# End of a sparse attention kernel: the last reciprocals' transpose ahead of the last context group, and the output chunks finished in another order

## The chip, the cores and the metric

One core of one Trainium2 chip runs the whole kernel in one launch. The metric is device time in microseconds (us) of the launch. TensorE (PE in the profile) does the matrix products, VectorE (DVE) and ScalarE (ACT) the elementwise work, GpSimd (POOL) issues the indirect transfers, SyncE (SP) the plain ones.

## The reference

For each of 16 batches of 1024 tokens with 512 features the kernel computes masked self-attention with one shared projection for queries, keys and values, and adds it to its input:

```python
xt = jnp.transpose(x, (0, 2, 1))                     # (16, 1024, 512)
q = xt @ Wq.T
qh = q.reshape(B, T, NH, dk).transpose(0, 2, 1, 3)   # 8 heads of 64
scores = scale * jnp.einsum('bhqd,bhkd->bhqk', qh, qh)
logits = (scores * cmask + (1.0 - cmask) * NEG) * rmask
attn = jax.nn.softmax(logits, axis=-1)
ctx = jnp.einsum('bhqk,bhkd->bhqd', attn, qh)
out = ctx.transpose(0, 2, 1, 3).reshape(B, T, D) @ Wo.T
return x + jnp.transpose(out, (0, 2, 1))
```

The mask holds zeros and ones and differs by batch; about half of the tokens are active. A row of a masked token has all logits equal, so its context is the mean of all queries.

## The kernel before, in words

The kernel gathers the active tokens of a batch into 512 to 544 slots and computes attention among those only; the masked tokens get one common row per batch, added in a pass of its own (line 888). All tokens go back to `y_out` by scatters, indirect transfers that POOL issues (line 901), 128 rows of 2 KB each.

Per batch, with the heads in four pairs p = 0 to 3:

- `scores` (line 701 for the products) computes a block of 128 queries against all slots for a head, and ScalarE takes the exponential and its row sums `z` (line 705).
- `attend` (line 726) multiplies the exponentials with the values. The context of one head pair is collected in one PSUM tile `pav`; the last 16 products of a pair are the context group, after which ScalarE copies the tile out as `c` (line 734).
- `recip_sums` (lines 749 to 758, DVE) makes the reciprocals of the row sums as columns in `rcol`. `recip_rows` turns them into rows: a TensorE transpose by the identity (line 764), a DVE copy `rr` out of PSUM (line 767), a small transfer to device memory `rd` (line 769, SP), and two transfers that read it back spread over 64 partitions each, `rb` (line 773, SP).
- `norm` (lines 799 to 803, DVE) multiplies `c` with `rb` and splits the result into two float16 parts, high and low, for the output product. In the last batch these are `xh` and `xl`.
- `product` (line 817) is the output product: for a chunk of 128 slots and each head pair e, three TensorE products (high x high weights, high x low weights, low x high weights), so twelve to a chunk. `plus` (line 822, DVE) adds the sum to the gathered input rows `xa`, and `scatter` sends them away.

Batches overlap: while batch b has its scores computed, the projections of b+1 and the output of b-1 are put between them by a list of pieces with costs (`run`). After the last batch nothing is left to overlap with, and `last` writes the end out by hand. Before the change it does this, in this order: the context group of the last head pair and all transfers still waiting; `recip_sums` of pair 3; the products of all four chunks for e = 0 to 2, nine for each chunk, with `recip_rows` behind chunk 0's; `norm` of pair 3; then for each chunk the three products for e = 3, `plus` and `scatter`. The four chunks' sums lie in two PSUM tiles `pss`, chunks 0 and 1 in the first and 2 and 3 in the second.

This is the order in which the program is written. A scheduler then orders each engine's instructions by priority and readiness as it expects them. `high_priority` moves a piece ahead, and `issue_after` (the helper `behind`, line 344) holds it behind a named instruction in that order, without a wait at run time. In the order that the scheduler built before the change TensorE does three products of chunk 0 (e = 0), the context group, the other six of chunk 0, the transpose of line 764, and nine each for chunks 1, 2 and 3; then for e = 3 the high products of chunks 0 and 2, the low ones of both, then chunk 1 and chunk 3. The order of `plus` and of the scatters is chunks 0, 2, 1, 3. Waits between engines are placed by tile: an instruction that writes any part of a tile waits for the earlier readers of the tile.

At the very end every engine loads a flag (line 1272) and branches (line 1273) over a general version of the kernel that is not executed with these inputs; POOL drains its transfers and the engines meet (line 1298).

Of the kernel before, what the change touches and what calls it, by code (L numbers as in the profile page):

```python
# [19 lines left out]
P = 128  # L20
# [5 lines left out]
DC = D // P  # L26
# [17 lines left out]
HPO = 300  # L44


class Fast:
# [344 lines left out]
    def rows(self, idx, tile):  # L392
        n = idx.shape[0]
        with self.behind(*self.pool):
            dma = self.nc.gpsimd.indirect_dma_start(out=tile[:n], out_offset=None, in_=self.x,  # L395
                                                    in_offset=bass.IndirectOffsetOnAxis(ap=idx, axis=0))
        self.once(dma, self.beat)
        self.pool = [dma.ins]
        return tile
# [360 lines left out]
    def recip_rows(self, b, p):  # L760

        nc, s = self.nc, self.st[b]
        pt = self.pm([P, P])
        nc.tensor.transpose(pt, self.rcol[p % 2], self.ident)
        rr = self.sb([10, P], F32, "rr", 2)
        with self.tc.high_priority(offset=HPO):
            nc.vector.tensor_copy(rr, pt[:10])
        rd = self.dram.tile([10, P], F32, tag="rd", name="rd")
        nc.sync.dma_start(out=rd, in_=rr)
        A = s["A"]  # L770
        rb = self.sb([P, C], F32, "rb", 2)[:, :A]
        for k in range(2):
            nc.sync.dma_start(out=rb[k * DK:(k + 1) * DK, :], in_=rd[5 * k:5 * k + 5, :].rearrange("k t -> (k t)")[:A]
                              .unsqueeze(0).broadcast_to([DK, A]))
        s.setdefault("rb", {})[p] = rb
# [33 lines left out]
    def product(self, ch, cl, cols, po=None, es=range(DC)):  # L809

        nc = self.nc
        if po is None:
            po = self.pm([P, D])
        wh, wl = self.w["o"]
        for e in es:
            for k, (a, w) in enumerate(((ch, wh), (ch, wl), (cl, wh))):
                nc.tensor.matmul(po[:cols.stop - cols.start], lhsT=a[:, e, cols], rhs=w[:, e, :],  # L817
                                 start=(e == 0 and k == 0), stop=(e == DC - 1 and k == 2))
        return po

    def plus(self, x, po):
# [88 lines left out]

    def last(self, b, todo):

        for f in self.soon + todo:
            f()
        self.soon = []
        while self.urgent or self.spare:
            self.issue()
        self.paced = False
        s = self.st[b]
        self.recip_sums(b, 3)  # L920
        pos = []
        for i in range(2):
            t = self.ps_s.tile([P, 2, D], F32, tag="s", name="pss")
            pos += [t[:, k, :] for k in range(2)]
        for i in range(4):
            self.product(s["ch"], s["cl"], slice(i * P, (i + 1) * P), pos[i], range(3))
            if i == 0:
                self.recip_rows(b, 3)
        self.norm(b, 3)
        for i in range(4):  # L930
            self.project(b, i, pos[i], range(3, DC))

    def run(self, flag):
        B = self.B
# [368 lines left out]
```

## Time and profile before

| what | us |
|---|---|
| median of three timed runs | 1032.48 |
| the three runs | 1032.48, 1032.27, 1036.74 |
| the profiled execution, its own time | 1036.56 |
| its span in the profile | 1034.9 |
| TensorE busy | 989.3 (96% of the span) |
| DVE busy | 724.1 (70%) |
| ACT busy | 659.2 (64%) |
| POOL busy | 301.5 (29%) |
| POOL's last scatter starts, after the span's start | 1029.88 |

The span is what the profile records from the first to the last instruction of one execution; the execution's own time is 1.66 longer. Starts in the timeline are counted from the span's start, and a line there reads: start, duration, engine, line of the kernel, operation, what it writes and reads, count; in brackets, how long the engine idled before it and what ended that. A name with q, as SPq or POOLq, is an engine's queue of transfers or its sequencer. TensorE's products are pipelined: a 128x512 product is recorded with 0.38 though one follows the other by about 0.22. The view of stretches gives for each one the engines' busy time with the number of instructions, then TensorE's granted clock as a share of full speed, the DMA engines' busy share and GB/s.

### The profile page before, as it was taken

The page shows a single profiled execution, that of the slowest core. Times are in us where ns is not written, and L with a number is a line of the kernel's source. Part 1 is how long each engine was busy: PE and PEld are TensorE (multiplying, and loading weights), DVE is VectorE, ACT ScalarE, POOL GpSimd, SP SyncE. Part 2 cuts the span into 40 slices and gives each one's busy share as a digit, 9 for nine tenths or more (in the row PEclk, how much of TensorE's full clock was granted, in tenths as well). Part 3 has the DMA queues.
Part 4 walks back from the last instruction along what each step waited for, and adds up shares of the span by engine and source line. Part 5 has one row for each costly group of instructions (what it writes and reads, how often), then busy time and mean ns, then how long its engine had stood idle before and what let it go on. Part 6 is the DMA issues. An engine that isn't in the chain of part 4 may idle for free. (4 is left out here: it accounts for less than half of the span.)

```text
span 1034.9 us, 23506 instructions
## 1 busy us (share of the span) xinstructions
PE 989.3 (96%) x8455; PEld 686.2 (66%) x8455; DVE 724.1 (70%) x2410; ACT 659.2 (64%) x1702; POOL 301.5 (29%) x307
## 2 busy tenths in 40 slices
PE   7798999999999999999999999999999999999996
PEld 6576667666676766767666676766767666676563
DVE  6897668676675667876676787767677776666653
ACT  5876667657667665667667567666667666565550
POOL 3101013222311232333232333323233232326562
PEclk9899999999999999999999999999999999999998
DMA  6846556557654485575658665576665657455652
GB/s 206 224 135 184 139 137 162 174 160 205 175 133 131 138 244 167 154 208 142 197 158 217 181 174 170 155 202 187 164 211 147 195 166 193 140 142 186 195 187 85
DMA packets 78795, 177.73 MB, mean 172 GB/s; under 512 B 14688, under 2 KB 20576, under 8 KB 78672
## 3 DMA queue, kind: packets, MB, share of 16 engines
q1 hardware_dynamic: 57584, 108.40, 39.0%
q0 software_dynamic: 21088, 67.75, 20.9%
q8 instruction: 69, 1.13, 0.5%
q14 instruction: 54, 0.44, 0.1%
HBM read 91.49 MB, written 33.91 MB: 121 GB/s over the span
## 5 line engine op out<-in xcount | busy, mean ns | idle before, releaser
L705 ACT ACTIVATE p<-pss,nm 128x528 f32<-128x528 f32 (+2 forms) x512 | 359.3, 706 | 186.5 <-PE pss L701 176.6
L701 PE MATMUL pss<-xx 128*128 128x264 f16 (+2 forms) x2048 | 302.7, 277 | 6.3 <-ACT p L705 5.2
L726 PE MATMUL pav<-p,v 128*64 128x264 f32 (+2 forms) x2048 | 243.3, 390 | 0.0
L701 PEld LDWEIGHTS <-xx 128*128 128x128 f16 x2048 | 194.9, 99 | 64.2 <-issue 26.2
L726 PEld LDWEIGHTS pav<-p,v 128*64 128x64 f32 x2048 | 141.5, 137 | 85.6 <-issue 13.5
L901 POOL DMA_INDIRECT y_out<-xa,idx x68 | 73.5, 1081 | 282.3 <-PE pss L701 100.1
L513 PE MATMUL pm<-xh,wqh 128*128 128x264 f16 (+5 forms) x512 | 142.4, 278 | 3.7 <-DVE xa L822 3.1
L513 PE MATMUL pm<-xh,wql 128*128 128x264 f16 (+5 forms) x512 | 141.9, 277 | 0.0
L513 PE MATMUL pm<-xl,wqh 128*128 128x264 f16 (+5 forms) x512 | 141.8, 277 | 0.0
L395 POOL DMA_INDIRECT xa<-x_in,idx x68 | 67.4, 992 | 208.2 <-PE pss L701 91.8
L513 PEld LDWEIGHTS <-wqh 128*128 128x128 f16 x1024 | 98.3, 99 | 23.7 <-issue 7.1
L705 ACT ACTIVATION_READ_ACCUMULATOR p<-pss,nm 128x1 f32 x512 | 104.1, 203 | 0.0
L901 POOL DMA_INDIRECT y_out<-xi,idx x60 | 73.6, 1226 | 96.7 <-PE pss L701 27.6
L817 PE MATMUL pm<-woh,ch 128*128 128x512 f16 x240 | 91.1, 380 | 0.0
L817 PE MATMUL pm<-wol,ch 128*128 128x512 f16 x240 | 91.0, 379 | 0.0
L817 PE MATMUL pm<-woh,cl 128*128 128x512 f16 x240 | 91.0, 379 | 0.0
L395 POOL DMA_INDIRECT xi<-x_in,idx x60 | 62.5, 1042 | 93.6 <-PE pss L701 31.2
L516 ACT ACTIVATE q<-pm 128x264 f32<-128x264 f32 (+5 forms) x128 | 50.1, 391 | 58.1 <-PE pm L513 57.4
L822 DVE SCALAR_TENSOR_TENSOR xa<-pm,xa 128x512 f32<-128x512 f32 x60 | 41.3, 688 | 54.3 <-PE pm L817 50.6
L817 PEld LDWEIGHTS <-ch 128*128 128x128 f16 x480 | 46.0, 98 | 44.8 <-issue 0.9
L888 DVE TENSOR_TENSOR xi<-xi,ub 128x512 f32<-128x512 f32 (+1 forms) x60 | 40.8, 687 | 42.6 <-PE pss L701 42.3
L799 DVE TENSOR_TENSOR c<-c,rb 128x528 f32<-128x528 f32 (+2 forms) x64 | 45.4, 709 | 30.0 <-PE pm L513 16.3
(223 smaller groups left out, 1506.4 us busy)
## 6 DMA issues: line engine op xcount, KB each, us to landing
xx<-hl SPq DMA_DIRECT2D x224, 136.0 KB
xm<-x_nat_in SPq DMA_DIRECT2D x56, 512.0 KB
rb<-rd SPq DMA_DIRECT2D x72, 132.0 KB
rb<-rd SPq DMA_DIRECT2D x40, 136.0 KB
pt<-c SPq DMA_DIRECT2D x36, 132.0 KB
pt<-p SPq DMA_DIRECT2D x36, 132.0 KB
ub<-ud SPq DMA_DIRECT2D x16, 256.0 KB
xx<-hl SPq DMA_DIRECT2D x32, 128.0 KB
```

The source lines that it names most:

```text
L395: dma = self.nc.gpsimd.indirect_dma_start(out=tile[:n], out_offset=None, in_=self.x, in_offset=bass.IndirectOffsetOnAxis(ap=idx, axis=0))
L513: self.beat = nc.tensor.matmul(pq, lhsT=w[:, c, e * P:(e + 1) * P], rhs=xx[:, c, cols], start=(k == 0), stop=(k == 3 * DC - 1)).ins
L516: nc.scalar.activation(s["q"][:, e, cols], pq, AF.Copy, scale=1.0 / (SX * SW))
L701: self.beat = nc.tensor.matmul(pt[:, g, :CH], lhsT=xx[:, 2 * k, i * P:(i + 1) * P], rhs=xx[:, 2 * k + a, g * CH:(g + 1) * CH], start=(a == ...
L705: self.exp = [nc.scalar.activation(t.rearrange("p (g c) -> p g c", g=2), pt[:, :, :CH], AF.Exp, bias=s["nm"][p // HG][:, p % HG:p % HG + 1 ...
L726: mm = nc.tensor.matmul(s["pav"][k * DK:(k + 1) * DK, g, :CH], lhsT=s["v"][p][:, i, k * DK:(k + 1) * DK], rhs=ps[k][:, cols], start=(i == ...
L799: self.once(nc.vector.tensor_tensor(c[:, :A], c[:, :A], s["rb"][p], ALU.mult), self.beat if p < 3 else None)
L817: nc.tensor.matmul(po[:cols.stop - cols.start], lhsT=a[:, e, cols], rhs=w[:, e, :], start=(e == 0 and k == 0), stop=(e == DC - 1 and k == 2))
L822: self.nc.vector.scalar_tensor_tensor(x, po, 1.0 / (SX * SW), x, ALU.mult, ALU.add)
L888: self.once(self.nc.vector.tensor_tensor(x[:n], x[:n], s["ub"][:n], ALU.add), self.beat)
L901: dma = self.nc.gpsimd.indirect_dma_start(out=self.out, out_offset=bass.IndirectOffsetOnAxis(ap=idx, axis=0), in_=x, in_offset=None)
```

## The change

Only `last` is rewritten, and two other functions keep a handle on the instruction that they issued last.

- `recip_sums` and `recip_rows` of pair 3 and the first six products of chunk 0 get high priority, and are written ahead of the last context group; `recip_rows` is held behind the sixth product, the context group and what else is left of the batch behind the transpose.
- Chunk 0's last three products for e = 2 and chunk 1's nine for e = 0 to 2 follow; chunks 2 and 3 get none at this point.
- After `norm`, chunks 0 and 1 are finished with e = 3. Chunks 2 and 3 are held behind them and computed in one piece each, all twelve products and then `plus` and `scatter`.

The number of instructions is the same on each engine. In the built order of the changed kernel TensorE does nine products of chunk 0, the transpose, the context group, nine of chunk 1, then for e = 3 chunk 0 and chunk 1, then twelve of chunk 2 and twelve of chunk 3. `plus` and the scatters go in the order 0, 1, 2, 3. Nothing else moves on any engine.

```diff
@@ recip_rows
-        nc.tensor.transpose(pt, self.rcol[p % 2], self.ident)
+        self.turn = nc.tensor.transpose(pt, self.rcol[p % 2], self.ident).ins
@@ product
-                nc.tensor.matmul(po[:cols.stop - cols.start], lhsT=a[:, e, cols], rhs=w[:, e, :],
-                                 start=(e == 0 and k == 0), stop=(e == DC - 1 and k == 2))
+                self.mm = nc.tensor.matmul(po[:cols.stop - cols.start], lhsT=a[:, e, cols], rhs=w[:, e, :],
+                                           start=(e == 0 and k == 0), stop=(e == DC - 1 and k == 2)).ins
@@ last
-        for f in self.soon + todo:
+        s = self.st[b]
+        rows = lambda i: slice(i * P, (i + 1) * P)
+        for f in self.soon:
             f()
         self.soon = []
-        while self.urgent or self.spare:
-            self.issue()
-        self.paced = False
-        s = self.st[b]
-        self.recip_sums(b, 3)
         pos = []
         for i in range(2):
             t = self.ps_s.tile([P, 2, D], F32, tag="s", name="pss")
             pos += [t[:, k, :] for k in range(2)]
-        for i in range(4):
-            self.product(s["ch"], s["cl"], slice(i * P, (i + 1) * P), pos[i], range(3))
-            if i == 0:
+        with self.tc.high_priority(offset=HPO):
+            self.recip_sums(b, 3)
+            self.product(s["ch"], s["cl"], rows(0), pos[0], range(2))
+            with self.behind(self.mm):
                 self.recip_rows(b, 3)
+        with self.behind(self.turn):
+            for f in todo:
+                f()
+        while self.urgent or self.spare:
+            self.issue()
+        self.paced = False
+        self.product(s["ch"], s["cl"], rows(0), pos[0], range(2, 3))
+        self.product(s["ch"], s["cl"], rows(1), pos[1], range(3))
         self.norm(b, 3)
-        for i in range(4):
+        for i in range(2):
             self.project(b, i, pos[i], range(3, DC))
+        with self.behind(self.mm):
+            for i in range(2, 4):
+                self.project(b, i, pos[i])
```

## The prediction

> **What bounds the kernel now.** The page comes first: TensorE is busy 96% of the span and 9 tenths or more in nearly every slice until the last, where its digit is 6. The change touches only the program's end; in the built order of both kernels every engine's instructions are the same up to the last batch's end. So I read the timeline from 1010 us on, then the DMA rows, then TensorE's granted clock. The timeline of before, cut to the chain of the last head pair's reciprocals (start, us, engine, line):
>
> ```profile
> 1011.77 3.67 PE L726 MATMUL pav<-p,v 128*64 128x256 f32 x32
> ...
> 1012.55 0.17 DVE L758 TENSOR_TENSOR rcol<-rcol,hit 128x10 f32<-128x10 f32 x1
> ...
> 1016.68 0.27 PE L764 MATMUL pm<-ident,rcol 128*128 128x128 f32 x1
> ...
> 1017.00 0.28 DVE L767 COPY rr<-pm 10x128 f32<-10x128 f32 x1 [4.27 <-PE pm L764]
> ...
> 1017.30 0.31 SPq L769 DMA_DIRECT2D rd<-rr  x1
> ...
> 1018.51 1.27 SPq L773 DMA_DIRECT2D rb<-rd  x2
> ...
> 1022.23 0.69 DVE L799 TENSOR_TENSOR c<-c,rb 128x512 f32<-128x512 f32 x1 [4.95 <-SPq L1273]
> ```
>
> The reciprocals are ready at 1012.72 (1012.55 + 0.17) but transposed at 1016.68, behind the context group and six products. From there two DMAs in a row, rd then rb, end at 1022.23 (SP's L1273 merely stands where rb landed). Then the end, PE, DVE and POOL of the same timeline:
>
> ```profile
> 1023.83 0.39 PE L817 MATMUL pss<-woh,xh 128*128 128x512 f16 x1 [1.04 <-DVE xh L802]
> ...
> 1024.70 0.60 PE L817 MATMUL pss<-woh,xl 128*128 128x512 f16 x2
> ...
> 1025.86 0.38 PE L817 MATMUL pss<-woh,xh 128*128 128x512 f16 x1 [0.57 <-DVE xa L822]
> ...
> 1025.12 1.29 DVE L822 SCALAR_TENSOR_TENSOR xa<-pss,xa 128x512 f32<-128x512 f32 x2 [0.62 <-PE pss L817]
> 1026.71 1.34 DVE L822 SCALAR_TENSOR_TENSOR xa<-pss,xa 128x512 f32<-128x512 f32 x2 [0.30 <-PE pss L817]
> ...
> 1026.08 0.96 POOL L901 DMA_INDIRECT y_out<-xa,idx  x1 [12.51 <-DVE xa L822]
> 1027.35 0.96 POOL L901 DMA_INDIRECT y_out<-xa,idx  x1 [0.30 <-issue]
> 1028.61 0.96 POOL L901 DMA_INDIRECT y_out<-xa,idx  x1 [0.30 <-issue]
> 1029.88 0.96 POOL L901 DMA_INDIRECT y_out<-xa,idx  x1 [0.31 <-issue]
> ```
>
> Once the first chunk is added (L822), POOL is the bound: four scatters 1.27 apart, the last at 1029.88. POOL's own drain ends at 1034.05, the span at 1034.9. So the end is the last scatter's start + 5.02.
>
> **The change part by part.** *The transpose moved up.* In the built order TensorE now does nine products of chunk 0 (e = 0 to 2), the transpose L764, the context group L726, nine products of chunk 1. Products follow each other by 0.216 (1021.33 to 1022.41: five steps in 1.08). Nine from 1011.03 end at 1012.97; their last operand is written at 1011.17 (L803, 1010.49 + 0.68) and rcol is ready at 1012.72, so nothing holds them. L764 starts at 1012.97 instead of 1016.68: **3.71 earlier**. The context group starts 0.20 behind it (as at 1001.24 to 1001.44), at 1013.17, 1.40 later than now; ScalarE's copy of it, 1015.49 now, ends at 1017.47. That is hidden behind rb, which lands later; without this cover it would cost 1.40. Chunk 1's nine products run from 1016.78 to 1018.72.
>
> *The two DMAs moved with it.* On SP they stand behind the same flag load as before (1012.1 to 1012.85); the copy rr would end at 1013.57, so SP is free. POOL's queue is unchanged. New is company: the scatter that POOL issues at 1012.60 still moves data (193 and 262 GB/s in 1013 to 1015; 16 GB/s after). From rd to rb SP waited 1.21 in the quiet (above), 1.45 at 994.23 just behind one scatter, 3.69 at 953.49 among several. I take 1.45, the row with one scatter: 0.24 lost. From rb to the multiply L799 it is 3.72 in the quiet and 5.20 among gathers (971.23 to 976.43); the scatter is over by then, so 3.72. L799 starts at T = 1022.23 - 3.71 + 0.24 = **1018.76**.
>
> *The end reordered.* Before, twelve products are left at T, three for each chunk; the other nine of chunks 2 and 3 ran while rd and rb were under way. Now they follow chunk 1, so thirty products stand behind T: 18 more, 18 x 0.216 = 3.9 of TensorE that lose their cover. The wait counts of the built program name two holds: chunk 1's first product behind T waits for chunk 0's L822, as it does now at 1025.86, and, new on this path, **chunk 3's first of all waits for chunk 2's L822**, because both chunks are halves of one tile. Queued behind these waits are all later products, and DVE and POOL behind them. From T, with before's own steps:
> - first product T + 1.60 (1023.83 - 1022.23); xl, written at T + 2.26, product at T + 2.40 (between 2.32 and 2.47);
> - L822 starts 0.42 after its last product (1024.70 to 1025.12) and takes 0.65: T + 2.82 to 3.47; POOL 0.31 later;
> - chunk 1 starts 0.09 after that (1025.77 to 1025.86), T + 3.56; its L822 T + 4.41 to 5.06, POOL T + 5.37, more than 1.27 after the first;
> - chunk 2 follows; its last product is 14 x 0.216 after T + 3.56, T + 6.58; L822 T + 7.00 to 7.65;
> - chunk 3 from T + 7.74, last product T + 10.12; L822 T + 10.54 to 11.19; **last scatter T + 11.50**.
>
> Before, the last scatter was T + 7.65 (1029.88 - 1022.23). So the end costs **3.85**, against 3.71 - 0.24 = 3.47 gained: + 0.38.
>
> *The tail* is kept at 5.02. The last scatter now goes alone; before, the last one's data flowed from about 1030.84 to 1032.2, and 256 KB at the 262 GB/s of 1030 to 1031 take 0.98, so between 0 and 0.4 may be gained; I take 0. The branch out of the program hides beside it: TensorE's takes 4.06 from 1027.0 and starts once the last hold is passed, about 1026.4 in both; DVE's drain comes 4.5 after the last L822 starts (1027.4 to 1031.9), so at 1033.8, against POOL's 1034.4: a cover of 0.6.
>
> **Sum.** Last scatter 1018.76 + 11.50 = 1030.26, span 1035.28 for 1034.9. The profiled execution took 1036.56, 4.08 above the median of the timed runs (1032.27, 1032.48, 1036.74). I carry the difference over: 1032.48 + 0.38 = **1032.9**.
>
> **Rivals.** *1. TensorE's clock falls (slower).* The granted clock changes on one grid of 3.41 us. Stretches of that grid, TensorE alone (busy, clock, DMA share, GB/s):
>
> ```profile
> 12.43:15.84 3.41, 1.19 (x15) 1.00 0.74 216
> 15.84:19.25 3.41, 3.41 (x27) 0.50 0.12 42
> 36.32:39.73 3.41, 0.64 (x6) 1.00 1.05 267
> 39.73:43.15 3.42, 2.64 (x20) 0.50 0.87 187
> 1022.77:1026.19 3.42, 1.81 (x9) 1.00 0.01 2
> 1026.19:1029.60 3.41, 1.13 (x6) 1.00 0.41 154
> 1029.60:1033.01 3.41, 0.00 (x0) 0.50 0.47 171
> ```
>
> The three stretches with a busy share of 0.35 or less are each followed by half clock; with 0.53 (1022.77) it stays full, and no other stretch is below that. In the changed kernel TensorE ends at 1018.89, works 0.60 from 1020.36 and 0.38 from 1021.16, and goes on at 1022.32: 0.98 of 3.41, **0.29**, if the grid falls there. Then the 15 products behind run at half speed for 3.41: + 1.7, 1034.6. It decides below a share between 0.35 and 0.53; at the middle, 0.44, a grid that starts within 0.5 of 1018.89 does it, 1.0 of 3.41, some 30%. On this execution's own grid (1019.36 to 1022.77) the share would be 0.42, undecided. The Trainium skill (TensorE: Matmul & The Clock Gate, section "Why this matters for your kernels") asks only for no idle gap above about 3 us. By that rule our longest gap would cost nothing and 1032.9 stands; the trace disagrees, since a gap of 2.27 ahead of 14.65 was followed by half clock.
>
> *2. rd and rb come late (slower).* At 3.69 and 5.20 they land 3.7 later than I take: 1036.6. Every microsecond counts, as TensorE already idles. Against it: only one scatter is in flight, not several.
>
> *3. A gain is left.* If chunk 3 isn't held, its products start 0.94 sooner: 1031.9. The wait count speaks against it. A lone scatter and quiet DMAs together give 1032.2 (0.4 and 0.24 less). That the transpose stays behind is excluded by the built order.
>
> **How the numbers follow.** Chances: forecast 0.55, clock 0.25, late DMAs 0.10, a gain 0.10. About 0.5% (5.2 us) is what a measurement of this kernel tells from no change; every case lies within it. Outside falls only a sum of late DMAs or a lower clock with a median from the upper group of runs (1036.7): slower 0.05; faster 0.01. Range: from 1031.5 (under rival 3, and the runs' 0.2) to 1037.1 (1036.74 + 0.38, which holds rivals 1 and 2). Early clock drops like the two shown (15.84 to 19.25 and 39.73 to 46.56, together 10.2 at half speed, so up to 5.1 lost), falling one way or another with the grid's chance, could make that spread; this is only argued.
>
> **What would show it.** Right: L764 near 1013, L799 near 1018.8, TensorE idle about 1.5 ahead of the first product, two holds by DVE's L822, scatters apart by 1.6, 2.6 and 3.5, the last near 1030.3. Wrong: chunk 3 starting straight behind chunk 2; rb landing past 1019.5; a granted clock of 0.5 between 1019 and 1030; DVE's or TensorE's drain behind POOL's.

## The result, and the profile after

| | runs | median, us | lowest to highest |
|---|---|---|---|
| before | 22 | 1035.78 | 1032.15 to 1041.03 |
| after | 22 | 1038.83 | 1036.07 to 1044.68 |

The ratio after to before is 1.0031, 95% interval 1.0018 to 1.0044: the changed kernel is slower by about 3.2 us (0.0031 x 1035.78), between 1.9 and 4.6. That is within the 0.5% that the prediction called "the same", but 1038.83 lies above its range. The kernel before, with 22 runs rather than three, has a median 3.30 above the 1032.48 from which the prediction started.

The profiled execution of after took 1039.73. Its page begins:

```profile
span 1037.9 us, 23506 instructions
```

The span was 1034.9 before. The two executions already differ by 0.85 where the end begins, ahead of anything that the change moves: chunk 0's first product starts at 1011.03 before and at 1011.88 after. So everything below is counted from that product, called S. The timeline of after (start, us, engine, line), cut to the chain:

```profile
1013.82 0.27 PE L764 MATMUL pm<-ident,rcol 128*128 128x128 f32 x1
...
1014.44 0.31 SPq L769 DMA_DIRECT2D rd<-rr  x1
1016.31 1.09 SPq L773 DMA_DIRECT2D rb<-rd  x2
...
1019.87 0.69 DVE L799 TENSOR_TENSOR c<-c,rb 128x512 f32<-128x512 f32 x1 [5.46 <-SPq L1282]
...
1021.47 0.39 PE L817 MATMUL pss<-woh,xh 128*128 128x512 f16 x1 [1.72 <-DVE xh L802]
...
1022.62 0.69 DVE L822 SCALAR_TENSOR_TENSOR xa<-pss,xa 128x512 f32<-128x512 f32 x1 [0.48 <-PE pss L817]
1023.37 0.38 PE L817 MATMUL pss<-woh,xh 128*128 128x512 f16 x1 [0.78 <-DVE xa L822]
...
1023.59 0.96 POOL L901 DMA_INDIRECT y_out<-xa,idx  x1 [9.18 <-DVE xa L822]
...
1025.18 0.96 POOL L901 DMA_INDIRECT y_out<-xa,idx  x1 [0.63 <-DVE xa L822]
...
1027.55 0.38 PE L817 MATMUL pss<-woh,xh 128*128 128x512 f16 x1 [0.78 <-DVE xa L822]
...
1027.77 0.96 POOL L901 DMA_INDIRECT y_out<-xa,idx  x1 [1.63 <-DVE xa L822]
...
1030.34 0.69 DVE L822 SCALAR_TENSOR_TENSOR xa<-pss,xa 128x512 f32<-128x512 f32 x1 [2.84 <-PE pss L817]
1031.31 0.96 POOL L901 DMA_INDIRECT y_out<-xa,idx  x1 [2.57 <-DVE xa L822]
```

The transpose is early, TensorE idles 1.72 ahead of the e = 3 products, both holds by DVE's L822 are there (0.78 idle each), and POOL, which before ran its scatters without a pause, now waits for each sum. Against S:

| us after S | before | after, predicted | after, measured |
|---|---|---|---|
| transpose L764 | 5.65 | 1.94 | 1.94 |
| rd issued to rb issued | 1.21 | 1.45 | 1.87 |
| multiply L799 | 11.19 | 7.73 | 7.99 |
| last scatter starts | 18.84 | 19.23 | 19.42 |
| span ends | 23.82 | 24.25 | 26.05 |
| last scatter to the end | 4.98 | 5.02 | 6.63 |

Of 2.23 lost between the two traces, 0.58 are there when the last scatter starts, and 1.65 arise behind it, where the kernel issues no more work. What happens there is seen in the stretches of 1 us (busy times, granted clock, DMA share and, last, GB/s). Before, from the last scatter's start at 1029.88:

```profile
1030.00:1031.00 1.00, 0.00 (x0) 0.00 (x0) 0.00 (x0) 0.00 (x0) 0.84 (x1) 0.50 0.72 262
1031.00:1032.00 1.00, 0.00 (x0) 0.00 (x0) 0.00 (x0) 0.00 (x0) 0.00 (x0) 0.50 0.67 258
1032.00:1033.00 1.00, 0.00 (x0) 0.00 (x0) 0.00 (x0) 0.00 (x0) 0.00 (x0) 0.50 0.16 49
```

After, from 1031.31:

```profile
1032.00:1033.00 1.00, 0.00 (x0) 0.00 (x0) 0.00 (x0) 0.00 (x0) 0.27 (x1) 1.00 0.22 74
1033.00:1034.00 1.00, 0.00 (x0) 0.00 (x0) 0.00 (x0) 0.00 (x0) 0.00 (x0) 1.00 0.57 205
1034.00:1035.00 1.00, 0.00 (x0) 0.00 (x0) 0.00 (x0) 0.00 (x0) 0.00 (x0) 1.00 0.07 16
1035.00:1036.00 1.00, 0.00 (x0) 0.00 (x0) 0.00 (x0) 0.00 (x0) 0.00 (x0) 0.65 0.02 8
```

Nearly all of the last scatter has landed by 1034, but 16 and 8 GB/s drip on for over a microsecond, a share of 0.07 and 0.02, about what one DMA engine of sixteen (0.06) gives. What still moves is in the DMA view of after, of 1034.5 to 1035.7 and then of 1033.1 to 1035.7 (packets, MB, busy share of the stretch):

```profile
q0 software_dynamic: 5, 0.02, 5.3%
```

```profile
q8 instruction: 1, 0.02, 3.3%
```

The five q0 packets, four of 4 KB and one of 4 bytes, are a sixteenth of the scatter's 80 packets. The q8 packet is 16 KB of *instructions*: by the trace's packet records it runs from 1033.18 to 1034.58, and the five follow it one after the other until 1035.56, with an 8 KB instruction packet (1034.61 to 1034.99) among them. The records don't name the DMA engine; that it is one and the same is read from this order. That fetch follows TensorE's branch out of the program (the rows of after's line 1282; before, it is line 1273):

```profile
L1282 PEldq COMPARE_BRANCH  x1: 3872/3872/3872, 1028.2 to 1028.2; - x1
```

```profile
L1273 PEldq COMPARE_BRANCH  x1: 4055/4055/4055, 1027.0 to 1027.0; - x1
```

In each trace one 16 KB fetch comes while this branch lasts and a second one 0.7 to 1.4 after its end. Before, the second fetch is the q8 packet of the DMA view of 1032.0 to 1033.5. It began at 1032.49, as the last packet of the last scatter landed, and it held nothing up:

```profile
q8 instruction: 1, 0.02, 4.0%
```

From there the theory and its rivals. **Fetch**: the second fetch gets ahead of the last scatter's share on one DMA engine. **Branch chain**: the end hangs on the engines' way out of the program; the last L822 ends 6.81 before the span's end before, 6.90 after, nearly the same. **Clock** and **late rd/rb** are the prediction's rivals; they are not in this trace (clock 1.00 until 1035.31), but could be in other executions.

### The profile page after: what moved, and what is told of

It is laid out like the page before. It is cut to its first block, busy times and chain, and to the rows that moved or that the text cites. A ratio compares the mean times of both kernels' runs of the same rounds, so it can differ in the third digit from the quotient of the medians.

```text
span 1037.9 us, 23506 instructions
## 1 busy us (share of the span) xinstructions
PE 989.9 (95%) x8455; PEld 685.9 (66%) x8455; DVE 724.3 (70%) x2410; ACT 659.3 (64%) x1702; POOL 301.2 (29%) x307
## 5 line engine op out<-in xcount | busy, mean ns | idle before, releaser
L822 DVE SCALAR_TENSOR_TENSOR xa<-pm,xa 128x512 f32<-128x512 f32 x60 | 41.3, 689 | 54.2 <-PE pm L817 50.6
L799 DVE TENSOR_TENSOR c<-c,rb 128x528 f32<-128x528 f32 (+2 forms) x64 | 45.5, 710 | 29.2 <-PE pm L513 16.3
```

Of the source, the lines that this page charges most:

```text
L799: self.once(nc.vector.tensor_tensor(c[:, :A], c[:, :A], s["rb"][p], ALU.mult), self.beat if p < 3 else None)
L822: self.nc.vector.scalar_tensor_tensor(x, po, 1.0 / (SX * SW), x, ALU.mult, ALU.add)
```

## The experiments

### Each half of the change alone

Transpose only: the rewritten start of `last`, and the end as before.

```diff
-        self.product(s["ch"], s["cl"], rows(1), pos[1], range(3))
+        for i in range(1, 4):
+            self.product(s["ch"], s["cl"], rows(i), pos[i], range(3))
         self.norm(b, 3)
-        for i in range(2):
+        for i in range(4):
             self.project(b, i, pos[i], range(3, DC))
-        with self.behind(self.mm):
-            for i in range(2, 4):
-                self.project(b, i, pos[i])
```

> The changed kernel with the end of before: the transpose stays ahead of the last context group, but all four chunks get their nine products before the last multiply, and are finished as before (chunks 0, 2, 1, 3). Counted from the first product of chunk 0: the multiply L799 at 8.0, as in the changed kernel (7.99; before 11.20). TensorE then has 27 products behind the context group and is late itself, so the first e = 3 product comes at about 11.6 and the last scatter at 17.6 (before 18.85, changed 19.43). Theory of the reordered end (the loss is in the 18 products that lost their cover and in the two holds): faster than before by about 1.2 us, faster than the changed kernel by 3.4. Rival, the transpose moved up is itself at fault (rd and rb landing among scatters, the context group late): no better than before, last scatter at 18.9 or later.

End only: `last` as before, with the products ahead of `norm` for chunks 0 and 1 alone.

```diff
-        for i in range(4):
+        for i in range(2):
             self.product(s["ch"], s["cl"], slice(i * P, (i + 1) * P), pos[i], range(3))
...
-        for i in range(4):
+        for i in range(2):
             self.project(b, i, pos[i], range(3, DC))
+        with self.behind(self.mm):
+            for i in range(2, 4):
+                self.project(b, i, pos[i])
```

> The transpose stays behind the context group as before, and only the end is in the new order (chunk 0, 1, then 2 and 3 in one piece). L799 at 11.2 after the first product of chunk 0, as before. TensorE idles some 4.4 us ahead of the first e = 3 product. Theory of the reordered end: last scatter 11.4 behind L799, so at 22.6, the program 3.8 us slower than before, or 5.3 if the last scatter is again caught by an instruction fetch. Theory of the clock: with a stretch of the 3.41 us grid nearly empty, the granted clock falls to 0.5 behind it and another 1.7 to 2.6 us are lost. Rival, the reordered end costs nothing: same as before.

*Transpose only*: L799 at S + 7.98, last scatter at S + 17.20 (before 18.84), end S + 21.95, so 1.87 earlier than before in the trace. The time doesn't confirm it: 1034.86 against 1035.25, ratio 1.0003 (0.9990 to 1.0016), at best 1.0 earlier. One trace is one execution; what makes up the difference stays open.

*End only*: slower, 1042.50 against 1035.25, ratio 1.0073 (1.0057 to 1.0089), 7.6 us; its trace ends at S + 30.99, 7.17 later than before. Here the clock takes part. TensorE idles 4.64 ahead of the e = 3 products (1025.55 in its timeline); the stretches of the clock's grid (PE busy first, granted clock third from the end):

```profile
1019.40:1022.81 3.41, 1.51 (x7) 0.49 (x5) 0.00 (x0) 0.00 (x0) 0.00 (x0) 1.00 0.17 63
1022.81:1026.22 3.41, 0.60 (x2) 0.11 (x2) 2.16 (x4) 0.00 (x0) 0.00 (x0) 1.00 0.06 20
1026.22:1029.64 3.42, 2.58 (x6) 0.82 (x7) 1.19 (x2) 0.00 (x0) 0.96 (x1) 0.50 0.07 28
1029.64:1033.05 3.41, 3.41 (x9) 1.18 (x8) 0.19 (x1) 0.00 (x0) 0.96 (x1) 0.50 0.33 126
1033.05:1036.46 3.41, 2.63 (x13) 1.10 (x12) 0.69 (x1) 0.00 (x0) 0.96 (x1) 1.00 0.09 31
```

A stretch with 0.44 busy (1.51 of 3.41) leaves the next at full clock; one with 0.18 is followed by two at half. So the reordered end alone is a clear loss; the early transpose is what makes it bearable, by shortening the idle time ahead of it.

### The holds taken away

Every chunk gets a PSUM tile of its own (the two `pss` tiles for chunks 0 and 1, the tiles `pm` of `project` for 2 and 3), so no product waits for a neighbour's L822:

```diff
-            pos += [t[:, k, :] for k in range(2)]
+            pos.append(t[:, 0, :])
...
-                self.project(b, i, pos[i])
+                self.project(b, i)
```

> The changed kernel, but each of the four chunks has a PSUM tile of its own, so that no chunk waits for the addition of the one before. The two holds of about 1.1 us each go. Counted from the first product of chunk 0: last scatter at about 17.2 (changed 19.43, before 18.85), last addition ends at 16.9. Two theories of the tail. Fetch: in the changed kernel the last scatter's packets on one DMA engine waited 1.6 us for a 16 KB instruction fetch; here the fetch comes some 5.4 us behind TensorE's branch, which is now early, so the last packet lands 2.6 behind the last scatter's start and the end comes at 22.3, faster than the changed kernel by 3.8 and than before by 1.6. Branch chain: the end comes 6.86 us behind the last addition's end, as it did in both kernels (6.85 and 6.87), so at 23.8: faster than the changed kernel by 2.2 and the same as before.

And with that, chunk 2's nine products too ahead of `norm`, where rd and rb cover them:

```diff
+        pos.append(self.pm([P, D]))
-        self.product(s["ch"], s["cl"], rows(1), pos[1], range(3))
+        for i in range(1, 3):
+            self.product(s["ch"], s["cl"], rows(i), pos[i], range(3))
         self.norm(b, 3)
-        for i in range(2):
+        for i in range(3):
             self.project(b, i, pos[i], range(3, DC))
         with self.behind(self.mm):
-            for i in range(2, 4):
-                self.project(b, i, pos[i])
+            self.project(b, 3)
```

> As the kernel with own tiles, but chunk 2's first nine products are done before the last multiply too, where TensorE idled 1.7 us in the changed kernel. Counted from the first product of chunk 0: scatters at about 11.9, 13.2, 14.4, 15.7, bound by GpSimd's 1.27 each; last addition ends at 15.3. Fetch theory of the tail: end at 20.7, faster than before by 3.2 us. Branch chain theory (6.86 behind the last addition): 22.1, faster than before by 1.7. If the scatters or the DMA queues were the bound and not the products, no gain over the kernel with own tiles.

> The kernel that does chunk 2's nine products early, once more beside the one with the gate, for a second execution's trace and more runs. Last scatter at 15.7, last packet 2.4 to 2.9 behind its start, end at 20.9 after chunk 0's first product; faster than before by 2 to 3 us. If the earlier trace was a lucky one, the last packet lands 4 us behind the last scatter here.

| | last L822 ends, S + | last scatter, S + | end, S + | ratio to before |
|---|---|---|---|---|
| after | 19.15 | 19.42 | 26.05 | 1.0031 (1.0018 to 1.0044) |
| own tiles | 16.90 | 17.18 | 22.52 | 0.9992 (0.9975 to 1.0008) |
| own tiles, chunk 2 covered | 15.41 | 15.68 | 20.86 | 0.9984 (0.9966 to 1.0003) |
| the same again | 15.35 | 15.63 | 21.01 | 0.9968 (0.9954 to 0.9983) |

Without the holds the last scatter starts 2.24 earlier than after's; with chunk 2 covered, 3.74 and 3.79 earlier. The timeline of the last one shows POOL nearly without a pause again:

```profile
1020.45 1.34 DVE L822 SCALAR_TENSOR_TENSOR xa<-pss,xa 128x512 f32<-128x512 f32 x2 [0.48 <-PE pss L817]
1021.41 0.96 POOL L901 DMA_INDIRECT y_out<-xa,idx  x1 [9.20 <-DVE xa L822]
1021.74 0.69 DVE L822 SCALAR_TENSOR_TENSOR xa<-pm,xa 128x512 f32<-128x512 f32 x1
1022.68 0.96 POOL L901 DMA_INDIRECT y_out<-xa,idx  x1 [0.31 <-DVE xa L822]
1023.94 0.96 POOL L901 DMA_INDIRECT y_out<-xa,idx  x1 [0.30 <-issue]
1024.33 0.69 DVE L822 SCALAR_TENSOR_TENSOR xa<-pm,xa 128x512 f32<-128x512 f32 x1 [1.90 <-PE pm L817]
1025.30 0.96 POOL L901 DMA_INDIRECT y_out<-xa,idx  x1 [0.40 <-DVE xa L822]
```

This version beats the kernel before, and after is slower than that: 1033.76 against 1037.87 in its second comparison, about 3.3 us (0.0032 x 1037.87); in the first comparison the interval just reaches past 1. And **the branch chain falls**: from the last L822's end to the span's end it is 5.62, 5.45 and 5.66 here, not 6.8 to 6.9.

### The branch taken away

The flag load, the branch and the general version behind it (not executed with these inputs) are left out, from before and from after:

```diff
-        bad = nc.values_load(flag, min_val=0, max_val=B)
-        with tc.If(bad > 0):
-            ...
-            general(tc, x, mask, wq_t, wo_t, out, B)
```

> The kernel before without its last part: the flag's load, the branch and the general version behind it are left out; that version is not executed with these inputs, so the output is the same, but for other inputs the kernel would be wrong. With it goes the branch over some thousand instructions and the 16 KB instruction fetches that follow it. Last scatter at 18.8 after chunk 0's first product, as before (18.84). Fetch theory of the tail: last packet 2.4 to 2.6 behind the last scatter's start and the end soon after; this is the reference for the changed kernel without branch, to be compared with it and not with before.

> The changed kernel without its last part, the same part left out as in the kernel before without branch (flag's load, branch and general version). Last scatter at 19.4 after chunk 0's first product (19.42 with the branch). Fetch theory of the tail (1.64 of the 2.23 us by which the changed kernel's end is late come from the last scatter's packets behind an instruction fetch): last packet 2.4 behind the last scatter's start instead of 4.26, and the end only about 0.6 us later than in the kernel before without branch. Rival, a lone last scatter or the reordered end is itself slower: the end stays 2.2 us later.

With no branch there is no instruction packet at the end, and the last scatter's last packet lands 2.36 (before) and 2.37 (after) behind its start: the difference of the tails, 4.26 against 2.62 with the branch, **is gone**. The last scatter of after without the branch, by the DMA view from 1035.4, just ahead of its start at 1035.41, to 1038 (40 slices of 0.065: busy tenths):

```profile
DMA  0000000000000000000000077899896976000000
...
q0 software_dynamic: 80, 0.26, 26.0%
```

All 80 packets go through in one block from 1036.9 on, the last at 1037.77. The times: 1034.61 (before) and 1036.68 (after) against 1037.87 with the branch in before, ratios 0.9974 (0.9954 to 0.9993) and 0.9992 (0.9978 to 1.0007). Their medians are 2.1 apart, where equal tails should have left 0.6, so part of the loss isn't the tail. With twelve runs each, that 2.1 isn't clearly less than the 3.2 with the branch: the traces show what the branch does to the tail, the times don't. This execution of after without the branch shows two other parts at once. SP's waits, of before, after and after without the branch (total, times, longest):

```profile
SPq L773 <- DMA rd<-rr: 0.8, 1, 0.8
```

```profile
SPq L773 <- DMA rd<-rr: 1.5, 1, 1.5
```

```profile
SPq L773 <- DMA rd<-rr: 3.2, 1, 3.2
```

rd was issued at 1015.35, shortly before the scatter of 1014.42 moved its data; a 16 KB instruction packet ran from 1016.23 to 1017.16 on one engine, and rd's last packet came at 1018.18, behind what waited there. rb went 3.54 behind rd, nearly the 3.69 of the prediction's second rival, but with one scatter in flight and an instruction packet, not with several scatters. TensorE then idled long enough for the first one:

```profile
1023.95 0.39 PE L817 MATMUL pss<-woh,xh 128*128 128x512 f16 x1 [2.87 <-DVE xh L802]
```

```profile
1022.33:1025.74 3.41, 1.00 (x3) 0.23 (x4) 2.79 (x5) 0.00 (x0) 0.00 (x0) 1.00 0.00 0
1025.74:1029.16 3.42, 3.31 (x8) 1.14 (x8) 0.75 (x2) 0.00 (x0) 1.82 (x2) 0.50 0.20 77
```

With 0.29 of the stretch busy (1.00 of 3.41), the clock was 0.50 in the next one, and the last scatter came 13.05 behind L799 rather than 11.43: + 1.6, as rival 1 said (+ 1.7). This execution took 1042.00, the median of the kernel's runs is 1036.68: it was not the usual one.

### The branch held back

If the fetch is what counts, moving it must move the tail. To the covered version a small transpose is added behind all products, which reads chunk 1's sum (in a second version chunk 0's, `s["xa"][0]`); TensorE's branch follows it.

```diff
             self.project(b, 3)
+        with self.behind(self.mm):
+            t = self.ps_av.tile([P, P], F32, tag="av", name="gate")
+            self.nc.tensor.transpose(t, s["xa"][1][:, :P], self.ident)
```

> The kernel that does chunk 2's nine products early, with one tiny product more behind all others, which waits for the addition of chunk 1 (it ends at 12.17 after chunk 0's first product). It changes nothing but the time at which TensorE comes to its branch: about 12.9 instead of 11.25, so its second instruction fetch moves from 15.4 to about 17.0, into the data of the last scatter (from 17.1 on). Fetch theory: same scatters (last at 15.7), last packet 3.9 to 4.3 behind the last scatter's start instead of 2.89, the end about 1.2 us later than without the gate. Rival, the fetch has nothing to do with it: the end as without the gate, within 0.3.

> As the kernel with the gate, but the tiny last product waits for the addition of chunk 0 (ends at 11.5 after chunk 0's first product) instead of chunk 1. The gate on chunk 1 put TensorE's branch at 12.89 and the second fetch at 18.13, too late: the last scatter's data was through. Here the branch comes at about 12.25 and the fetch, asked for 0.74 behind the branch's end, at 16.4 to 17.1, just ahead of the last scatter's data (from 17.1). Fetch theory: last packet 3.5 to 4.2 behind the last scatter's start (2.89 and 3.02 without the gate, 2.96 with the later one). Rival, no effect of the fetch: 2.9 to 3.0 again.

The first missed its aim: waiting for chunk 1's sum, the branch came so late that the second fetch began 2.51 behind the last scatter's start, behind its data; the last packet landed at 2.96, as without the transpose (2.89 and 3.02), so it tells nothing for or against (ratio 0.9969, 0.9953 to 0.9986). The second, waiting for chunk 0's sum, put the fetch from 1.01 to 2.36 behind the scatter's start, and the last packet landed at 3.36: later than without, by 0.3 to 0.5, but short of the 3.5 to 4.2 expected, since the fetch came earlier than in after and ended earlier. It is a single trace.

### Further executions of both kernels

> The changed kernel once more, for the trace of a second execution. Fetch theory: the last scatter's last packet again about 4 behind its start, with a 16 KB instruction packet ahead of the rest; end at 26.0 after chunk 0's first product if L799 is at 8.0 and the clock stays. With rd caught by a fetch, L799 at 9.5; with the 3.41 us grid falling on the idle stretch, the clock at 0.5 behind it and the last scatter 1.6 later. If the first trace's tail was an accident: last packet 2.4 behind the scatter's start, end at 24.2.

> The changed kernel a third time. The same alternatives as for the second look: tail of 4 us (fetch theory) or 2.4 (accident), L799 at 8.0 or 9.5, clock at full speed or at half behind the idle stretch.

> The kernel before once more, for the trace of a second execution. Rd goes out when no scatter is under way: L799 at 11.0 to 11.3 after chunk 0's first product. Last scatter at 18.8, last packet 2.4 to 2.7 behind its start, since TensorE's second fetch comes at about 21.5, behind the data; end at 23.8. If the fetch comes some tenths sooner here, the tail is 4 and the end at 25.4: then before is exposed as the changed kernel is.

Two more profiled executions of after and one of before, unchanged. These three and the gate on chunk 0 are one execution each, on another chip, where two executions of before took 1049.79 and 1043.04, those of after 1046.71 and 1048.28 and the gate 1046.40. So their times tell nothing, and only their traces are used. With these, the order of branch, fetch and scatter can be laid side by side for all twelve traces of kernels with the branch and the two without. All times are us behind the last scatter's start; its data, where nothing is in the way, run from 1.55 to about 2.35:

| trace | branch ends | second fetch | last packet |
|---|---|---|---|
| chunk 2 covered | -1.02 | -0.27 to 0.97 | 2.89 |
| the same again | -0.71 | 0.08 to 1.12 | 3.02 |
| own tiles | -0.37 | 0.37 to 1.67 | 2.96 |
| gate on chunk 0 | 0.25 | 1.01 to 2.36 | **3.36** |
| after, second execution | 0.54 | 1.27 to 2.94 | **3.93** |
| end only | 0.73 | 1.47 to 2.54 | **3.41** |
| after | 0.77 | 1.88 to 3.27 | **4.26** |
| after, third execution | 0.99 | 1.74 to 3.28 | **4.27** |
| before | 1.23 | 2.62 to 3.58 | 2.62 |
| before, second execution | 1.30 | 2.57 to 3.53 | 2.57 |
| gate on chunk 1 | 1.33 | 2.51 to 3.60 | 2.96 |
| transpose only | 1.48 | 2.39 to 3.36 | 2.40 |
| before and after, no branch | none | none | 2.36, 2.37 |

A fetch that begins 1.0 to 1.9 behind the scatter's start goes first, and the held share lands 0.87 to 1.00 after the fetch ends (3.27 + 0.99 = 4.26; 2.94 + 0.99 = 3.93). In seven traces the second fetch begins 0.73 to 0.79 behind the branch's end. In before, its second execution, transpose only and gate on chunk 1 it begins later than that (0.91 to 1.39), at 2.39 to 2.62, when the scatter's other packets are through: it stands behind the scatter and costs nothing. One that ends before 1.55 is past. Own tiles lies on the edge, with a fetch that ends at 1.67: one chain of five packets lands at 2.80 there, another at 2.96. The four values of 2.9 to 3.0 come with an instruction packet of 8 KB that lies at 1.5 to 2.4, in the scatter's data; by the same order it should be the cause, but no run takes it away alone. From the last packet to the end it is 2.2 to 2.4 in all fourteen traces. So the end follows the last packet, not the branch.

## Why the prediction was right and wrong

**The transpose**: right, S + 1.94 as predicted, and the context group behind it stayed covered.

**rd and rb**: the mechanism was right (one scatter in flight delays rd), the size too small: 1.86 to 1.88 in the three traces of after, not 1.45. In the first of them rd's packets run from 1015.68 to 1015.79, together with the last packets of the scatter that POOL issued at 1013.45. A 16 KB instruction packet was under way too (until 1015.73), but what stood behind it was a sixteenth of the scatter (until 1016.72) and nothing of rd. From rb to L799 it was 3.56, not 3.72. Together L799 is 0.26 late.

**The reordered end**: right. L822's holds are where the prediction put them, the last scatter starts 11.43 behind L799 for 11.50, the scatters follow each other by 1.59, 2.59 and 3.54 (1.6, 2.6, 3.5). The end costs 3.78 for 3.85; the early L799 gains 3.20 for 3.47.

**The step that failed is the tail**: "The tail is kept at 5.02 ... between 0 and 0.4 may be gained; I take 0". It measured 6.63, with 6.31 and 6.65 in the other two executions, against 4.98 and 4.96 in the two traces of before. The prediction looked at the branch only as something that has to end before POOL's drain, and there it was right: the branch ends long before. It didn't ask what the branch sets in motion. After it instructions are fetched over the DMA engines that also carry the last scatter, and the change moved the branch's end from 1.23 to 0.77 behind the scatter's start, from harmless into the window. A row for it stood in the trace of before: an instruction packet at 1032.49, right behind the last packet.

**Rival 1, the clock**, did not happen in the three traces of after, where the stretch on the grid was 0.50 busy in the profiled one and 0.50 and 0.49 in the others, but its mechanism and price (1.6 for 1.7) are shown in the version without the branch and, dearer (14.29 from L799 to the last scatter), in the end alone. **Rival 2, late rd**, happened in the version without the branch too, at nearly its size but by an instruction packet. **Rival 3, a gain**, did not: chunk 3 waits for chunk 2's L822 as the wait count said.

**The sum**: the three traces of after end at S + 26.05, 25.58 and 25.97, the two of before at 23.82 and 23.64: 2.1 on average, of which 0.4 was predicted and most of the rest is the tail. The timed difference is 3.2 (1.9 to 4.6), which takes the 2.1 in. Where the other microsecond comes from stays open. It may come from executions with late rd and a lower clock, as the one without the branch; how often they occur was not counted. It may also lie ahead of S, which came at 1011.03 in before and 1011.88 in after, and on the other chip at 1017.70 and at 1019.33 and 1020.52; but S came anywhere from 1008.09 to 1013.55 in the versions of the experiments, which differ only in the end, so these few traces don't decide it. The number itself missed for a second reason. 1032.48 was the median of three runs of a kernel whose 22 runs centre at 1035.78; 0.38 above that would have been 1036.16, within the range, and the tail is what carries it out.

## What to carry to other kernels

When the end of a program moves, look in the DMA view for instruction packets and set their time against the last transfer's data: a branch that engines take near the end starts fetches that can hold up one sixteenth of a transfer, and the whole transfer with it. A PSUM tile shared by two chunks turns "finish one, then the next" into a wait for the first one's reader; give the chunks tiles of their own, and put under a transfer's wait every product that does not need it. With runs that spread by 9 us, take the base from as many as there are, and judge a change of 3 us by counting from a common point inside the traces as well.

## What the runs showed of the hardware

**Instruction fetches share the DMA engines with data.** In the last 40 us of the traces a 16 KB packet takes 0.9 to 1.7 us. What stands behind it is late, though most of the transfer has long landed: the scatter's last packet comes at 3.4 to 4.3 instead of 2.4, and rd's wait in the version without the branch was 3.2 instead of the 1.5 in after. TensorE's branch itself takes 3.4 to 4.3 in all twelve traces that have it. The Trainium skill (Runtime: NRT & Kernel Launch, section "Instruction fetch mechanics") says that a sequencer fetches blocks of 16 KiB over a DMA queue, and that a taken branch beyond the pages it holds has to fetch its target before it goes on. The traces agree with both; the page counts the cost as a stall of the branching engine, while here it fell on another engine's transfer.

**The clock follows a grid of 3.41 us, and an idle gap of less than 3 us can be enough to halve it.** In the rows above, shares of 0.44 and 0.50 of a stretch were followed by full clock, 0.29 and 0.18 by half, and in the prediction's rows 0.35 by half. That doesn't make a sharp bound between 0.35 and 0.44: elsewhere in the traces 0.43 (own tiles, 11.14 to 14.55), 0.45 (before, second execution, 984.41 to 987.82), 0.52 (gate on chunk 0, 10.71 to 14.12) and once even 0.70 (after, second execution, 172.88 to 176.29) were followed by half clock, and 0.43 (before, second execution, 1032.20 to 1035.61) by full. Below 0.4, half clock always followed in the fourteen traces; above that, the share as the profile shows it doesn't settle it alone. The stretch with 0.29 was followed by one stretch at half clock, that with 0.18 by two; while the clock is at half, what ended it was a stretch with a share of 0.97 or 1.00, and one with 0.76 did not. The Trainium skill (TensorE: Matmul & The Clock Gate, section "Why this matters for your kernels") asks for no idle gap above about 3 us; the gap that reaches into the 0.29 stretch was 2.87, and the clock fell all the same.
